# A decoder layer: the order of all engines written out from the first instruction

## The chip, the cores and the metric

The kernel runs on one core of one Trainium2 chip. The metric is the time of one execution in microseconds of the device, median of several runs. A profile is one further execution, recorded by the hardware; its span runs from the first to the last instruction.

The engines are called PE (matmuls), DVE (vector), ACT (activations, scalar), POOL (general) and SP (issues transfers). PEld is PE's loading of weights.

## The reference

One pre-norm decoder layer on x of 32 sequences of 128 tokens, width 128, in float32:

```
x = x + attn(layernorm(x))                 # 16 heads of 8, linear attention: sigmoid(q), sigmoid(k),
                                           # kv = sum k v, num / den, layernorm, gate (h + beta), Wo, relu
x = x + xattn(layernorm(x), ctx_768)       # 16 heads of 64, softmax over 128 context tokens of width 96
x = x + ffn(layernorm(x))                  # a shared SwiGLU, and one of 8 routed experts per token
```

## The kernel before, in words

The 32 sequences are eight groups of four (`x0` to `x7`, tiles of 128 tokens x 4 x 128). For each group there are two short chains and then eight steps:

- `attention(g)`: statistics of x (`st_a`, `mv_a`, `var_a` on DVE, `rstd_a` on POOL), `xn_a`, transposed on PE (`xnTp_a`) and copied by ACT (`xnT_a`); keys and values `kvp` and queries `qp` on PE; the state `stp`, masked into `st_a`; `ndp`, divided into `att`; a second norm (`st_n`, `rstd_n`, `xn_n`, `lnTp`, `lnT`), the gate `hp` and `gT`, `op`, and the sum into x.
- `prologue(g)`: statistics of the new x (`st_b`, `rstd_b`), `xn_b`, transposed (`xnTp_b`, `xnT_b`), and for groups after the first also the context (`eTp`, `eT`).
- the steps. A step is one sequence and one half of the heads of the cross attention, 64 in all. `keys` (`xkp`) and `queries` (`xqp`) of blocks of 128 columns are made four steps ahead into the tiles `qk`; `scores` (`sc`), their maxima (`nmax` on DVE), eight exponentials (`pr` on ACT), `divide` (`rs` on DVE, `pr` times `rs` on POOL), `turn` (`prTa`, `prTb` on PE, copied by DVE and ACT), `values` (`vp`, `v`), `mix` (`avp`, `oT`), `project` (`xyp`, added to x).

The chains are generators that yield a letter at each stage; `place("M", "P")` and the like advance all that wait at such a letter. In the steps every call goes through `InTurn` (line 19), which keeps the order of the program on each engine, by ordering each instruction behind the one before. Ahead of the steps, `InTurn` is off (`on` is set only behind the first queries), and there the scheduler of the framework orders the instructions of each engine by itself. So it is the scheduler that puts `hb_c` ahead of `xn_a` on DVE, that mixes the statistics of two groups, and that sets the second group's `kvp` ahead of the first group's `ndp` on PE.

Before the steps the old program makes all eight keys of group 0 (evicted by ACT), runs `attention(0)` and `prologue(0)`, and `attention(1)` and `prologue(1)` beside them, one stage behind; of group 1 only `eTp`, `xnTp_b` and their evictions are left for step 0.

The loads: SP issues x0, x1, eg0 (the context), wk_x, then small columns (bh, beta, lnw, lnb), wo, bo, wq_x, wv_x, wo_x, bo_x, eg1 and the other x; ACT issues the weights of the first attention (two halves of `wkv_a`, two of `bkv_r`, `wq_a`, `bq_c`). Transfers share a small ring of semaphores, so an issue can wait until an earlier transfer that used the same semaphore has landed.

After the steps come the shared and the routed feed-forward network, which the change does not touch.

Of the kernel before, what the change touches and what calls it, by code (L numbers as in the profile page):

```python
# [12 lines left out]
ALU = mybir.AluOpType  # L13
AX = mybir.AxisListType

P = 128
# [25 lines left out]
def kernel(  # L42
# [31 lines left out]
    nc = tc.nc  # L74
    B, S, D = x.shape
    DE = enc.shape[2]
    INNER = c_wq.shape[1]
# [6 lines left out]
    GT = 4  # L84
# [24 lines left out]
    def bank(name):  # L109
        return ps_mm.tile([P, 512], F32, tag="mm", name=name)  # L110
# [1 line left out]

    xg = []

    def load_x(g):
        t = const.tile([P, GT, D], F32, tag=f"x{g}", name=f"x{g}")
        nc.sync.dma_start(
            out=t, in_=x[g * GT : (g + 1) * GT].rearrange("b s d -> s b d")
        )
        xg.append(t)  # L120

    load_x(0)
    load_x(1)


    ident = const.tile([P, P], F32, tag="ident", name="ident")
# [58 lines left out]
    def column(src, name, queue):  # L185
        t = wa.tile([P, 1], F32, tag=name, name=name)
        queue.dma_start(out=t, in_=src.rearrange("(p o) -> p o", o=1))
        return t
# [6 lines left out]
    def load_e(g):  # L195
        if g < NG:
            t = pe.tile([P, GT, DE], F32, tag="eg", name=f"eg{g}")
            nc.sync.dma_start(
                out=t, in_=enc[g * GT : (g + 1) * GT].rearrange("b s d -> s b d")
            )  # L200
            eg_of[g] = t

    load_e(0)
    wk_x = const.tile([DE, INNER], F32, tag="wk_x", name="wk_x")
    nc.sync.dma_start(out=wk_x, in_=c_wk)
    wh_a = wa.tile([P, D], F32, tag="wh_a", name="wh_a")
    nc.sync.dma_start(out=wh_a, in_=a_wh)
    bh_c = column(a_bh, "bh_c", nc.sync)
    beta_c = column(a_beta, "beta_c", nc.sync)
# [6 lines left out]
    hb_c = wa.tile([P, 1], F32, tag="hb_c", name="hb_c")  # L216

    def late_constants():
        nc.vector.tensor_reduce(
            hsel, ident.rearrange("p (i h) -> p h i", h=HA), AX.X, ALU.add  # L220
        )
        nc.vector.tensor_copy(
            hmask.rearrange("p (i h) -> p i h", h=HA),
            hsel.unsqueeze(1).to_broadcast([P, DA + 1, HA]),
        )
        nc.vector.tensor_tensor(hb_c, bh_c, beta_c, ALU.add)

    wq_x = const.tile([P, INNER], F32, tag="wq_x", name="wq_x")  # L230
# [6 lines left out]
    nc.sync.dma_start(out=bo_x, in_=c_bo.partition_broadcast(P))  # L237
    load_e(1)
    for g in range(2, NG):
        load_x(g)  # L240


    gw_f = const.tile([P, NE], F32, tag="gw_f", name="gw_f")
# [61 lines left out]
    def unordered(ins, done, why):  # L305
# [9 lines left out]
    pe_, dve, act_, pool_ = (  # L315
        InTurn(tc, e) for e in (nc.tensor, nc.vector, nc.scalar, nc.gpsimd)
    )
# [14 lines left out]
    def normalized(src, of, pool, name):  # L332
        mv, rstd = of
        xn = pool.tile([P, GT, D], F32, tag="xn", name=f"xn_{name}")
        for t in range(GT):
            dve.tensor_scalar(
                xn[:, t, :],
                src[:, t, :],
                mv[:, t, 0:1],
                rstd[:, t : t + 1],  # L340
                ALU.subtract,
                ALU.mult,
            )
        return xn

    def transposed(src, n, rows, name):

        ps = bank(name)
        for t in range(n):
            pe_.transpose(ps[0:rows, t * P : (t + 1) * P], src[:, t, :], ident)  # L350
        return ps
# [8 lines left out]
    def attention(g):  # L360
# [66 lines left out]
        for a in range(2):  # L427
            nd2 = bank(f"ndp{g}_{a}")[:, 0 : 2 * W].rearrange("p (b w) -> p b w", b=2)
            for b in range(2):
                t = 2 * a + b  # L430
# [21 lines left out]
        yield "E"  # L452
        an = normalized(att, of, pa, f"n{g}")
        yield "P"
        lnp = transposed(an, GT, P, f"lnTp{g}")
        hp = bank(f"hp{g}")
        pe_.matmul(hp, lhsT=wh_a, rhs=xnT, start=True, stop=True)
        yield "E"
        lnT = pa.tile([P, GW], F32, tag="lnT", name=f"lnT{g}")
        act_.activation(lnT, lnp, AF.Identity, bias=lnb_c, scale=lnw_c)  # L460
# [28 lines left out]
    eT_of, xnT_of, qk_of = {}, {}, {}  # L489

    def encoder(g, evict):

        eT = pe.tile([DE, GW], F32, tag="eT", name=f"eT{g}")
        eT_of[g] = eT
        evict(eT, transposed(eg_of[g], GT, DE, f"eTp{g}")[0:DE, :])
        load_e(g + 2)

    def prologue(g):

        xr = xg[g]  # L500
        yield "S"
        of = statistics(xr, f"b{g}")
        yield "M"
        xn = normalized(xr, of, pe, f"b{g}")

        pool_.tensor_tensor(
            xr, xr, bo_x.unsqueeze(1).to_broadcast([P, GT, D]), ALU.add
        )
        yield "P"
        if g not in eT_of:  # L510
            ep = transposed(eg_of[g], GT, DE, f"eTp{g}")
        xp = transposed(xn, GT, P, f"xnTp_b{g}")
        yield "E"
        if g not in eT_of:
            eT_of[g] = pe.tile([DE, GW], F32, tag="eT", name=f"eT{g}")
            dve.tensor_copy(eT_of[g], ep[0:DE, :])
            load_e(g + 2)
        xnT_of[g] = pe.tile([P, GW], F32, tag="xnT", name=f"xnT_b{g}")
        act_.copy(xnT_of[g], xp)

    def keys(g, s, j, evict):

        cols = slice((4 * s + j) * P, (4 * s + j + 1) * P)
        t = pq.tile([P, 2, GW], F32, tag="qk", name=f"qk{g}_{s}_{j}")
        kp = bank(f"xkp{g}_{s}_{j}")
        pe_.matmul(kp, lhsT=wk_x[:, cols], rhs=eT_of[g], start=True, stop=True)
        evict(t[:, 1, :], kp)
        qk_of[g, s, j] = t

    def queries(g, s, j):  # L530

        cols = slice((4 * s + j) * P, (4 * s + j + 1) * P)
        qp = bank(f"xqp{g}_{s}_{j}")
        pe_.matmul(qp, lhsT=wq_x[:, cols], rhs=xnT_of[g], start=True, stop=True)
        act_.activation(qk_of[g, s, j][:, 0, :], qp, AF.Copy, scale=QSCALE)
# [54 lines left out]
    def divide(k):  # L590
        pr = pr_of[k].rearrange("p a j k -> p (a j) k")
        rs = small.tile([P, 8], F32, tag="rs", name=f"rs{k}")
        dve.reciprocal(rs, sums_of.pop(k))
        pool_.tensor_tensor(
            pr, pr, rs.unsqueeze(2).to_broadcast([P, 8, P]), ALU.mult
        )
# [363 lines left out]
    beside = []  # L960

    def begin(work, then=None):
        beside.append([next(work), work, then])

    def place(*which):
        for at in which:
            for one in list(beside):
                if one[0] == at:
                    one[0] = next(one[1], None)
                    if one[0] is None:  # L970
                        beside.remove(one)
                        if one[2] is not None:
                            begin(one[2]())


    begin(attention(0), lambda: prologue(0))
    place("S")
    late_constants()
    tick = 0
    while beside and 0 not in xnT_of:  # L980
        place("M", "P")
        if tick == 0:
            encoder(0, act_.copy)
            begin(attention(1), lambda: prologue(1))
        else:
            k = tick - 1
            keys(0, k // 4, k % 4, act_.copy)
        place("E", "S")
        tick += 1
    for k in range(tick - 1, 8):  # L990
        keys(0, k // 4, k % 4, act_.copy)
    for j in range(4):
        queries(0, 0, j)

    for engine in (pe_, dve, act_, pool_):
        engine.on = True
    for i in range(len(steps)):
        place("E")
        if i >= 1:
            divide(i - 1)  # L1000
        if i + GT < len(steps):
            if steps[i + GT] not in qk_of:
                keys(*steps[i + GT], dve.tensor_copy)
            queries(*steps[i + GT])
        place("S")
        if i >= 2:
            mix(i - 2)
        scores(i)
        if i >= 3:
            project(i - 3)  # L1010
            if i % 8 == 2:
                begin(router(steps[i - 3][0]))
        place("M")
        if i >= 1:
            turn(i - 1)
        values(i)
        place("P")
        if i % 8 == 3:
            clear_sorted(i // 8)
            g = i // 8 + 2  # L1020
            if g < NG:
                begin(attention(g), lambda g=g: prologue(g))
        if i == 12:
            load_ffn()
        if i == len(steps) - 4:

            first_part.close()
            pools["g"] = ctx.enter_context(tc.tile_pool(name="pg", bufs=2, side="right"))
            pools["c"] = ctx.enter_context(tc.tile_pool(name="pc", bufs=4, side="right"))
            pd = ctx.enter_context(tc.tile_pool(name="pd", bufs=1, side="right"))  # L1030
            pools["down"] = pd.tile([P, NC, NE, D], F32, tag="wdr", name="wdr")
# [10 lines left out]
    n = len(steps)  # L1042
# [136 lines left out]
```

## Time and profile before

| | us |
|---|---|
| median of six runs | 692.55 |
| lowest and highest run | 688.79 and 695.77 |
| the profiled execution | 692.75 |
| its span | 691.0 |
| first matmul starts | 10.23 |
| first matmul of the first scores starts | 44.82 |
| scores of steps 1, 2, 3, 4 start | 50.24, 57.16, 64.08, 71.06 |
| PE busy in the span | 627.8 |

In the timeline a row has the start in us, the duration, the engine, the line, the operation with what it writes and reads, and in brackets the idle time of the engine before it and what ended it. Most operations bear line 30 or 35, the line of `InTurn` that issues them, so rows are told apart by the names of tiles. In the view by stretches, a row has the stretch, its length, and then for PE, PEld, DVE, ACT and POOL the busy time and the number of instructions; behind them the clock granted to PE, the share of the transfer engines that is busy, and GB/s. The granted clock is recorded from its first change on; before that the view shows 1.00.

The chain that ended last runs through PE for 61% of the span, DVE 22%, ACT 7%.

### The profile page before, as it was taken

The page shows a single profiled execution, that of the slowest core. Times are in us where ns is not written, and L with a number is a line of the kernel's source. Part 1 is how long each engine was busy: PE and PEld are TensorE (multiplying, and loading weights), DVE is VectorE, ACT ScalarE, POOL GpSimd, SP SyncE. Part 2 cuts the span into 40 slices and gives each one's busy share as a digit, 9 for nine tenths or more (in the row PEclk, how much of TensorE's full clock was granted, in tenths as well). Part 3 has the DMA queues.
Part 4 walks back from the last instruction along what each step waited for, and adds up shares of the span by engine and source line. Part 5 has one row for each costly group of instructions (what it writes and reads, how often), then busy time and mean ns, then how long its engine had stood idle before and what let it go on. Part 6 is the DMA issues. An engine that isn't in the chain of part 4 may idle for free.

```text
span 691.0 us, 13411 instructions
## 1 busy us (share of the span) xinstructions
PE 627.8 (91%) x4699; PEld 456.8 (66%) x4699; DVE 473.0 (68%) x1265; ACT 335.4 (49%) x1319; POOL 251.5 (36%) x237
## 2 busy tenths in 40 slices
PE   4888999999999999999999999899999789898895
PEld 2545677676667666766676667576766556598873
DVE  3755767878787868786878687867766747444443
ACT  3365654564556465646564557454554531133330
POOL 2132323424342434342424342434252342145552
PEclk9999999999999999999999999999999989899999
DMA  7999700000000000000000000002000000688628
GB/s 178 336 327 371 277 2 1 12 1 9 9 13 1 9 9 12 1 9 9 12 2 13 5 2 1 13 11 56 1 17 1 1 13 5 181 244 251 201 63 219
DMA packets 48258, 50.12 MB, mean 73 GB/s; under 512 B 9232, under 2 KB 33296, under 8 KB 48192
## 3 DMA queue, kind: packets, MB, share of 16 engines
q1 hardware_dynamic: 41888, 42.65, 20.1%
q0 software_dynamic: 2272, 4.72, 2.0%
q10 hardware_dynamic: 4032, 1.90, 1.1%
q8 instruction: 37, 0.61, 0.4%
q14 instruction: 29, 0.24, 0.1%
HBM read 24.60 MB, written 26.76 MB: 74 GB/s over the span
## 4 chain that ended last, share of the span: by engine, by line
PE 61%; DVE 22%; ACT 7%; issue 3%; DMA 2%; SPq 2%; POOL 1%; ACTq 0%; DVEq 0%; POOLq 0%
PE sc L35 8%; PE avp L35 8%; PE xyp L35 6%; ACT pr L35 6%; PE rgu L35 5%; PE xkp L35 5%; PE vp L35 5%; PE xqp L35 5%; DVE nmax L35 4%; PE ryp L35 3%; PE prTa L35 2%; PE prTb L35 2%; DVE x L35 2%; PE kvp L35 2%; SPq L298 1%
## 5 line engine op out<-in xcount | busy, mean ns | idle before, releaser
L35 ACT ACTIVATE pr<-sc,nmax 128x128 f32<-128x128 f32 x512 | 180.1, 378 | 187.7 <-DVE nmax L35 187.1
L35 POOL TENSOR_TENSOR pr<-pr,rs 128x1024 f32<-128x1024 f32 x64 | 121.4, 1896 | 211.7 <-DVE rs L35 78.9
L35 ACT ACTIVATION_READ_ACCUMULATOR pr<-sc,nmax 128x1 f32 x512 | 110.7, 216 | 0.0
L35 PEld LDWEIGHTS avp<-prT,v 128*64 128x64 f32 x1024 | 58.6, 137 | 65.5 <-issue 25.0
L35 PE MATMUL avp<-prT,v 128*64 128x128 f32 x1024 | 77.9, 281 | 13.8 <-ACT prT L35 13.8
L35 DVE TENSOR_REDUCE nmax<-sc 128x8 f32<-128x1024 f32 x63 | 76.9, 1220 | 16.9 <-PE sc L35 16.9
L35 PE MATMUL sc<-qk 64*128 64x128 f32 x1024 | 75.3, 287 | 0.7 <-ACT pr L35 0.7
L35 PE MATMUL xyp<-wo_x,oT 128*128 128x128 f32 x512 | 73.8, 288 | 0.0
L35 PEld LDWEIGHTS sc<-qk 64*128 64x128 f32 x1024 | 62.9, 189 | 13.1 <-issue 10.8
L35 DVE COPY oT<-avp 128x512 f32<-128x512 f32 x64 | 44.0, 688 | 34.6 <-PE avp L35 34.4
L35 PEld LDWEIGHTS xyp<-wo_x,oT 128*128 128x128 f32 x512 | 61.9, 191 | 7.7 <-issue 0.4
L35 PE MATMUL vp<-wv_x,eT 96*128 96x512 f32 x128 | 65.7, 594 | 0.0
L35 PE MATMUL xkp<-eT,wk_x 96*128 96x512 f32 x112 | 58.1, 600 | 7.1 <-DVE eT L35 7.1
L35 PE MATMUL xqp<-xnT_b,wq_x 128*128 128x512 f32 x118 | 60.9, 597 | 0.0
L35 DVE COPY v<-vp 128x512 f32<-128x512 f32 x64 | 43.8, 684 | 18.8 <-PE vp L35 18.7
L35 POOL DMA_INDIRECT xsort<-xs,row x32 | 32.6, 1018 | 58.0 <-issue 38.2
L35 POOL DMA_INDIRECT ytok<-yt,rows x39 | 37.3, 958 | 41.0 <-DVE rows L35 40.7
L35 PE MATMUL prTa<-ident,pr 128*128 128x128 f32 x256 | 38.9, 275 | 11.3 <-POOL pr L35 11.3
L35 ACT ACTIVATE qk<-xqp 128x512 f32<-128x512 f32 x59 | 36.5, 619 | 25.7 <-PE xqp L35 25.7
L35 DVE COPY prT<-prTa 128x512 f32<-128x512 f32 x64 | 43.9, 685 | 6.2 <-PE prTa L35 3.6
L35 DVE COPY qk<-xkp 128x512 f32<-128x512 f32 x56 | 36.5, 651 | 11.6 <-PE xkp L35 11.5
L35 ACT COPY prT<-prTb 128x512 f32<-128x512 f32 x64 | 39.8, 622 | 3.8 <-PE prTb L35 3.8
(213 smaller groups left out, 1009.8 us busy)
## 6 DMA issues: line engine op xcount, KB each, us to landing
xsort<-zeros SPq DMA_DIRECT2D x66, 264.0 KB
wt<-wall SPq DMA_DIRECT2D x39, 256.0 KB
xt<-xsort SPq DMA_DIRECT2D x39, 66.0 KB
x<-in_x_dram SPq DMA_DIRECT2D x8, 256.0 KB
eg<-in_ctx_dram SPq DMA_DIRECT2D x8, 192.0 KB
out_dram<-x SPq DMA_DIRECT2D x6, 256.0 KB
wall<-in_L_ffn_rt_gate_dram SPq DMA_DIRECT2D x1, 1024.0 KB
wall<-in_L_ffn_rt_up_dram SPq DMA_DIRECT2D x1, 1024.0 KB
```

What stands on the lines that cost most here:

```text
L35: self.last = make(*operands, **more)
L298: ins = nc.sync.dma_start(out=xsort[r : r + n].rearrange("(p k) d -> p k d", p=P), in_=zeros)
```

## The change

Four things are changed, all ahead of or in the first steps:

1. `InTurn` is on from the first instruction, so that the order of the program holds on PE, DVE, ACT and POOL from the start. `late_constants` goes through `dve`, and `hb_c` leaves it for a later place.
2. That order is written out call by call. The context's transposes (`encoder`) and key 0 stand first on PE, ahead of the transposes of the first rows; the first group's chain stands in front; keys 1 to 3 and the second group's stages are set between its stages. The second group comes only to its `ndp` before the first queries; the rest of it (`att`, `xn_n`, `hp`, `lnTp`, `gT`, `op`, the whole `prologue(1)`) is put into the list `beside`, and the steps 0 to 3 advance it. Keys 4 to 7 of group 0 are no longer made ahead: steps 0 to 3 make them, as the later steps do, with eviction by DVE.
3. x0 is loaded in two halves, one from SP and one from ACT; wk_x in two halves of columns; x1 goes behind both.
4. In `attention`, `hp` stands ahead of `lnTp`, for all groups.

```diff
-    def load_x(g):
+    def load_x(g, *queues):
         t = const.tile([P, GT, D], F32, tag=f"x{g}", name=f"x{g}")
-        nc.sync.dma_start(
-            out=t, in_=x[g * GT : (g + 1) * GT].rearrange("b s d -> s b d")
-        )
+        n = GT // len(queues)
+        for k, queue in enumerate(queues):
+            queue.dma_start(
+                out=t[:, k * n : (k + 1) * n],
+                in_=x[g * GT + k * n : g * GT + (k + 1) * n].rearrange(
+                    "b s d -> s b d"
+                ),
+            )
         xg.append(t)
-    load_x(0)
-    load_x(1)
+    load_x(0, nc.sync, nc.scalar)
...
-    nc.sync.dma_start(out=wk_x, in_=c_wk)
+    for k in range(2):
+        half = slice(k * INNER // 2, (k + 1) * INNER // 2)
+        nc.sync.dma_start(out=wk_x[:, half], in_=c_wk[:, half])
+    load_x(1, nc.sync)
...
-        nc.vector.tensor_tensor(hb_c, bh_c, beta_c, ALU.add)
...
-        lnp = transposed(an, GT, P, f"lnTp{g}")
         hp = bank(f"hp{g}")
         pe_.matmul(hp, lhsT=wh_a, rhs=xnT, start=True, stop=True)
+        lnp = transposed(an, GT, P, f"lnTp{g}")
...
-    begin(attention(0), lambda: prologue(0))
-    place("S")
+    for engine in (pe_, dve, act_, pool_):
+        engine.on = True
+
+    def whole(g):
+        yield from attention(g)
+        yield from prologue(g)
+
+    def key(k):
+        keys(0, k // 4, k % 4, act_.copy)
+
+    one, two = whole(0), whole(1)
+    next(one), next(two)
+    next(one)
+    encoder(0, act_.copy)
+    key(0)
+    next(one)
+    next(one)
+    next(one)
+    next(two)
+    key(1)
+    next(one)
+    next(one)
     late_constants()
-    tick = 0
-    while beside and 0 not in xnT_of:
-        place("M", "P")
-        if tick == 0:
-            encoder(0, act_.copy)
-            begin(attention(1), lambda: prologue(1))
-        else:
-            k = tick - 1
-            keys(0, k // 4, k % 4, act_.copy)
-        place("E", "S")
-        tick += 1
-    for k in range(tick - 1, 8):
-        keys(0, k // 4, k % 4, act_.copy)
+    next(two)
+    key(2)
+    next(one)
+    next(two)
+    next(one)
+    next(two)
+    key(3)
+    next(one)
+    dve.tensor_tensor(hb_c, bh_c, beta_c, ALU.add)
+    next(two)
+    next(one)
+    next(one)
+    next(two)
+    next(one)
+    next(one)
+    next(two)
+    next(one)
+    next(two)
+    next(one)
+    next(two)
+    next(one)
+    next(one)
+    next(one)
+    next(one)
+    next(one, None)
     for j in range(4):
         queries(0, 0, j)
-
-    for engine in (pe_, dve, act_, pool_):
-        engine.on = True
+    beside.append(["E", two, None])
```

More of the change, by code (lines that the diff above doesn't have):

```diff
@@ L218, in late_constants @@
     def late_constants():
-        nc.vector.tensor_reduce(
+        dve.tensor_reduce(
             hsel, ident.rearrange("p (i h) -> p h i", h=HA), AX.X, ALU.add
         )
-        nc.vector.tensor_copy(
+        dve.tensor_copy(
             hmask.rearrange("p (i h) -> p i h", h=HA),
@@ L239 @@
     for g in range(2, NG):
-        load_x(g)
+        load_x(g, nc.sync)
     gw_f = const.tile([P, NE], F32, tag="gw_f", name="gw_f")
```

## The prediction

> **What bounds the kernel now.** I read the page first, then the timeline of the first 80 us by engine, then PE's busy time and granted clock in short stretches.
>
> ```profile
> span 691.0 us, 13411 instructions
> PE 627.8 (91%) x4699; PEld 456.8 (66%) x4699; DVE 473.0 (68%) x1265; ACT 335.4 (49%) x1319; POOL 251.5 (36%) x237
> ...
> PE   4888999999999999999999999899999789898895
> ```
>
> PE is 91% busy, and from about 70 us on it hardly stops (steps of 7 to 9 us). The change adds and removes no PE work, so it can only gain where PE idles or waits in a wrong order: before the first scores (44.82 us) and in the first steps. Whatever lead exists at step 8 is kept to the end, since the order after that is the same.
>
> Timeline of the stretch before the steps (start, duration, engine, line):
>
> ```profile
> 9.55 0.16 DVE L226 TENSOR_TENSOR hb_c<-bh_c,beta_c 128x1 f32<-128x1 f32 x1 [2.45 <-DMA beta_c<-in_L_attn_beta_dram]
> ...
> 17.80 0.95 DVE L30 TENSOR_TENSOR st_a<-stp,hmask 128x288 f32<-128x288 f32 x2 [2.28 <-PE stp L30]
> ...
> 31.77 1.11 DVE L30 TENSOR_SCALAR xn_n<-att,mv_n,rstd_n 128x128 f32<-128x128 f32 x4 [1.12 <-POOL rstd_n L30]
> ```
>
> ```profile
> 10.23 1.25 PE L30 MATMUL xnTp_a<-ident,xn_a 128*128 128x128 f32 x4 [10.23 <-DVE xn_a L30]
> ...
> 18.09 1.89 PE L30 MATMUL kvp<-wkv_a,xnT_a 128*128 128x256 f32 x8
> 19.82 1.02 PE L30 MATMUL qp<-xnT_a,wq_a 128*128 128x512 f32 x2
> 20.67 1.02 PE L30 MATMUL xkp<-eT,wk_x 96*128 96x512 f32 x2
> 21.54 1.15 PE L30 MATMUL ndp<-st_a,qT_a 128*128 128x144 f32 x8
> ```
>
> Three self-made delays of the first group: DVE sat 2.45 us behind `hb_c`, with `xn_a` behind it; `ndp`, ready at 18.8, stood on PE behind the second group's `kvp`, `qp` and a key until 21.54; `ob`, ready at 31.8, stood on DVE behind the second group's `xn_n` until 32.80.
>
> **Part by part: the way to the first scores.** Durations are pitches, start to start: a 512-column matmul 0.86 us, `kvp` 1.73, `stp`/`ndp` 0.98, `op` 0.88, four transposes 0.44; before 13.5 us PE ran at half of that (an `eTp` transpose 421 ns, at 46 us 272 ns).
>
> - Start to `kvp`. Before: 12.15. After: two halves of x come by two queues, est. 3.8 instead of 4.11; statistics in strict order take 1.9 (group 2 at 70.22 to 72.11), `rstd` 1.04, so `xn_a` starts at 6.7 and not 9.84. But PE now first does `eTp` and key 0, and waits for eg (before: landed about 6.3 behind two x; now behind half an x, est. 5.2), for ACT and for half of wk_x. On ACT, bq_c's issue waits in the built program for wkv_a's first half, which x's half now precedes, so the table load (1.28) starts at est. 5.3 instead of 4.05, and `eT` is copied at 6.6 to 7.2. Key 0 at half rate 1.72: 8.9; `xnTp_a` 0.87 to 9.8; copy 0.6; key 1, 1.72, runs beside it to 11.6. `kvp` at 11.6: **-0.55**. Bounds: eg and wk_x no earlier than before (8.9) gives +1.8; no wait at all -2.0.
> - `kvp` to `ndp`: before 9.39. After: `kvp` 1.73, bias 0.69, `ks` 0.62, `stp`, mask 0.95, key 3: 6.6, part at half rate. **-2.8**.
> - `ndp` to `op`: 9.08 before; without the mixing of `hp`, `lnTp` and `xn_n`, but with strict statistics (+0.3), 8.0. **-1.1**.
> - `op` to `xnTp_b`: 7.35; without `xn_n` (1.0) and the second `gT` in the way 5.8. **-1.55**.
> - `xnTp_b` to `xqp`: 2.36; without key copies in the way on ACT 1.75. **-0.6**.
> - `xqp` to scores: 4.49; one key more on PE: 6 x 0.86 = 5.16. **+0.7**.
>
> Sum -5.9: first scores at 38.9. The other loads cost nothing: wq_x was issued at 9.17 and is needed at 33.8; SP's later waits (x1 on eg, wh_a to lnb on ACT's loads) have 3 to 15 us of slack; if x1 came after 10.5, `kv_a` would be late by as much. POOL's order is unchanged. `hp` ahead of `lnTp` in later groups: 0, `lnT` stands behind exponentials anyway (lnTp done 115.0, lnT at 116.52).
>
> **What the steps give back.** Steps 0 to 3 get four keys (3.44), `hp`, `lnTp`, `op` (2.18); `eTp` and `xnTp_b` go from step 0 to step 3. Step 0: DVE does the second group's statistics before the row maxima: +0.3. Step 1, 6.92 before (scores at 50.24, 57.16): `prTa` starts 2.2 after the scores, then 0.87 + 0.86 + 0.86 + 0.44 + 0.86 + 0.86 + 1.03 = 5.8, so 8.0: +1.1. Step 2: ACT's chain of exponentials still ends last: 0. Step 3, 6.98: PE's first key of group 1 waits for `eT1`, which DVE copies behind `oT`, maxima, `xn_b`, `prT` and `v`, 6.1 after the scores; then 0.86 + 0.86 + 1.03: 8.8, +1.85. Sum **+3.2**. Without a change of clock the lead is 5.9 - 3.2 = **2.7 us**.
>
> **The clock.** Stretches of 3.41 us; columns PE busy, PEld, DVE, ACT, POOL, granted clock:
>
> ```profile
> 34.84:38.25 3.41, 1.43 (x11) 1.25 (x11) 2.15 (x10) 0.59 (x1) 1.01 (x1) 1.00 0.86 267
> ...
> 61.29:64.70 3.41, 1.78 (x26) 1.47 (x26) 0.71 (x2) 2.22 (x10) 1.85 (x1) 1.00 0.99 356
> ...
> 563.05:566.46 3.41, 1.05 (x11) 0.95 (x10) 1.54 (x3) 0.00 (x0) 3.21 (x3) 1.00 0.06 20
> 566.46:569.87 3.41, 3.41 (x6) 0.98 (x4) 0.44 (x1) 1.18 (x2) 1.13 (x2) 0.50 0.12 40
> 586.94:590.35 3.41, 1.26 (x5) 0.57 (x3) 3.17 (x12) 0.60 (x1) 2.50 (x4) 1.00 0.12 40
> 590.35:593.77 3.42, 2.79 (x13) 2.79 (x14) 1.18 (x2) 0.00 (x0) 0.82 (x1) 0.50 0.51 140
> 593.77:597.18 3.41, 3.41 (x7) 1.71 (x7) 0.69 (x1) 0.60 (x1) 0.00 (x0) 0.50 0.63 193
> ```
>
> The half-clock stretches lie on one grid of 3.41 us with the rise at 13.5 us. Twice a stretch with 1.05 and 1.26 us of PE work was followed by half clock; once with 2.79 the half clock stayed; 1.78 kept the full clock. (A third drop, at 552.8, follows a stretch that is busy on paper, with 0.95 us of it `lp`, eight-column matmuls.) The reader should see that sparse PE work costs the *next* 3.4 to 6.8 us.
>
> The keys that the change takes away were PE's filling. In the new order PE has, from the end of `ndp` of group 1 (28.1) to the first `xqp` (33.8), only four transposes, 0.44 us in 5.7. On any grid one stretch there holds under 1.05. So I expect half clock over the six matmuls before the scores: one stretch costs 1.7, two 3.4; the first begins with a wait, like 590.35, so I take **3.3** (0 to 4.3). Again in steps 0 and 1, where PE waits 2 us for the exponentials, does scores (1.09), waits 1.1 for `pr`: about 1.2 in a stretch; this event falls on step 1, now PE-bound: **2.4** (0 to 3.4). In step 0 of before `eTp` and `xnTp_b` filled that hole.
>
> The Trainium skill ("TensorE: Matmul & The Clock Gate", Part 1 and "HAM oscillation") halves PE's clock after a wholly idle window of about 3.4 us and warns of PE gaps above that. By this rule the gap before the scores (3.9 us) trips it and the holes of 1 to 2 us in the steps do not: the sum would be +0.6 instead of +3.0. The rows above trip with 1.05 and 1.26 us of work in the stretch, so I follow them.
>
> Against the profiled execution (692.75 us: span 691.0 and 1.75 around it) the sum is -2.7 + 3.3 + 2.4 = +3.0, 695.75. But its grid was kind to the old order: a stretch began at 10.09, just before the first matmul at 10.23, and the sparse 34.84 to 38.25 (1.43) was cut in two. On another grid the old kernel pays, too: on average 0.85 at the start and some 1.7 to 3.4 in 4 of 10 positions, about 2.1 in all (0 to 3.4). The median of the six runs (692.55, from 688.79 to 695.77) stands for mixed grids: 692.55 + 3.0 - 2.1 = 693.45, rounded to **693.3 us**.
>
> **Rivals.**
> 1. *Lead eaten by steps and clock, no change* (above): 693.3. For it: no PE work goes away; a 5.7 us hole in PE. Against: the thresholds rest on three events. Chance 0.60.
> 2. *The clock holds*, or only one short event comes while the old kernel pays its own: -2.7, with the 2.1 saved -4.8: 687.8 to 689.9. For it: 1.78 busy did not trip. Against: the hole is far emptier than that. Chance 0.20, most of it over 0.5%.
> 3. *Slower by half clock*: both holes cost two full stretches, 2 x 3.4 = 6.8, and the old kernel pays nothing: 692.75 - 2.7 + 6.8 = 696.9. It decides as soon as clock losses exceed 2.7 + 3.5 = 6.2 us beyond those of before. Chance 0.20.
>
> That the order isn't as written is excluded: the built program's queues show it.
>
> **How the numbers follow.** 0.5% (3.46 us) is about what a measurement of this kernel can tell from no change. Faster by more: 0.16, mostly rival 2; slower by more: 0.20, rival 3 and late eg or wk_x (+1.8); between: 0.64. Range 688.4 to 697.0: from the middle of rival 2 to rival 3.
>
> **What would show it.** First matmul at 5 to 5.5 us, `kvp` of group 0 near 11.6, `ndp` near 18, first `xqp` near 33.5; PEclk of about 0.5 somewhere in 31 to 40 and again in 47 to 57; scores at about 42 rather than 39; step 3 of 8.8 us. Wrong if PEclk is 1.00 from 14 us on: then the lead at step 8 is near 2.7. Wrong, too, if key 0 starts after 8.5.

## The result and the profile after

| | before | after |
|---|---|---|
| median, us | 692.71 (80 runs, 688.79 to 695.77) | 694.52 (38 runs, 692.66 to 696.94) |
| ratio to before, 95% interval | | 1.0026 (1.0018 to 1.0034) |
| mean granted clock of an execution, averaged | 0.9894 (30 executions) | 0.9839 (40 executions) |
| first scores start | 44.82 | 41.61 |
| scores of steps 1, 2, 3, 4 | 50.24, 57.16, 64.08, 71.06 | 47.47, 58.50, 65.42, 74.28 |
| profiled execution, its span | 692.75, 691.0 | 693.39, 691.6 |

The change made the kernel 0.26% slower: less than the 0.5% that the chances go by, but outside the interval. The page of the profile after, at the places that were shown of before:

```profile
span 691.6 us, 13415 instructions
PE 630.0 (91%) x4699; PEld 458.4 (66%) x4699; DVE 477.3 (69%) x1269; ACT 333.8 (48%) x1315; POOL 251.4 (36%) x237
...
PE   6689999999899989999999999999998879798895
...
PEclk9978999999999999999999999999999999999999
```

The same instructions on PE are busy 2.2 us longer, and the row of the clock has a dent in its third and fourth slice (34 to 69 us), where before it had none. Timeline of the way to the first scores, DVE and then PE:

```profile
16.16 0.95 DVE L35 TENSOR_TENSOR st_a<-stp,hmask 128x288 f32<-128x288 f32 x2 [0.65 <-PE stp L35]
17.02 0.15 DVE L35 TENSOR_TENSOR hb_c<-bh_c,beta_c 128x1 f32<-128x1 f32 x1
...
27.25 0.69 DVE L35 TENSOR_TENSOR ob<-op,bo_a 128x512 f32<-128x512 f32 x1 [0.52 <-PE op L35]
```

```profile
11.26 1.89 PE L35 MATMUL kvp<-wkv_a,xnT_a 128*128 128x256 f32 x8
...
17.75 1.15 PE L35 MATMUL ndp<-st_a,qT_a 128*128 128x144 f32 x8
...
32.12 1.25 PE L35 MATMUL xnTp_b<-ident,xn_b 128*128 128x128 f32 x4 [3.93 <-DVE xn_b L35]
34.05 5.91 PE L35 MATMUL xqp<-xnT_b,wq_x 128*128 128x512 f32 x8 [0.68 <-ACT xnT_b L35]
39.80 1.02 PE L35 MATMUL xkp<-eT,wk_x 96*128 96x512 f32 x2
...
53.15 1.91 PE L35 MATMUL hp<-xnT_a,wh_a 128*128 128x512 f32 x2
...
71.26 1.12 PE L35 MATMUL xkp<-eT,wk_x 96*128 96x512 f32 x2 [0.98 <-DVE eT L35]
```

The three self-made delays are gone: `hb_c` waits for nothing, `ndp` of the first group stands at 17.75 instead of 21.54, `ob` waits only for its own `op`. The first queries begin 6.28 us earlier (34.05 against 40.33). But the eight passes of the four query matmuls take 5.91 us where before they took 3.70, `hp` in step 1 takes 1.91 where a matmul of that size takes 1.02, and in step 3 PE waits 0.98 for `eT` of the second group.

The view by stretches on this run's own grid of 3.41 us (PE, PEld, DVE, ACT, POOL busy, then the granted clock):

```profile
28.30:31.71 3.41, 0.00 (x0) 0.00 (x0) 2.09 (x10) 0.00 (x0) 1.01 (x1) 1.00 1.00 359
31.71:35.12 3.41, 2.32 (x6) 1.29 (x7) 2.50 (x8) 0.59 (x1) 1.27 (x1) 0.50 1.03 370
35.12:38.53 3.41, 3.41 (x6) 1.34 (x5) 0.00 (x0) 1.19 (x2) 0.00 (x0) 0.50 0.98 312
38.53:41.95 3.42, 3.42 (x14) 1.46 (x14) 1.06 (x4) 1.43 (x3) 0.00 (x0) 1.00 1.01 290
45.36:48.77 3.41, 1.35 (x17) 0.97 (x16) 1.59 (x6) 2.54 (x13) 1.04 (x1) 1.00 1.06 402
48.77:52.19 3.42, 2.51 (x9) 2.10 (x10) 1.82 (x2) 2.25 (x13) 0.85 (x1) 0.50 1.06 387
52.19:55.60 3.41, 3.41 (x8) 1.64 (x7) 0.69 (x1) 1.12 (x5) 0.00 (x0) 0.50 1.06 387
```

Twice PE goes through a sparse stretch (0.00 and 1.35 us of work) and is then granted half clock for two stretches: over the first queries, and over step 1. These are the two clock events of what follows. From 55.6 on the clock is full until 567.6. So the lead that the written order could have at the first scores (predicted 5.9 us; 5.40 in e3 below, where the clock stays full) becomes 3.21, and at the scores of step 4 the new kernel is 3.22 behind.

Behind that it stays behind: the transposes ahead of the last router start at 543.25 before and at 546.51 after. Of these 3.26 us, 2.6 come back in the last fifth, which the change does not touch: there, ahead of the last 2 us, half clock is recorded for 13.65 us before (552.80 to 556.21, 566.45 to 569.87, 590.35 to 597.17) and for 6.83 after. Which stretches fall there differs from run to run, so the single pair of spans (0.6 us apart) says less than the medians (1.8 apart).

### The profile page after: what moved, and what is told of

Read it like the earlier page. It is cut to its first block, busy times and chain, and to the rows that moved or that the text cites. A ratio compares the mean times of both kernels' runs of the same rounds, so it can differ in the third digit from the quotient of the medians.

```text
span 691.6 us, 13415 instructions
## 1 busy us (share of the span) xinstructions
PE 630.0 (91%) x4699; PEld 458.4 (66%) x4699; DVE 477.3 (69%) x1269; ACT 333.8 (48%) x1315; POOL 251.4 (36%) x237
## 4 chain that ended last, share of the span: by engine, by line
PE 61%; DVE 24%; ACT 7%; issue 4%; POOL 2%; DMA 1%; ACTq 0%; DVEq 0%; POOLq 0%
PE sc L35 7%; PE avp L35 7%; PE xyp L35 6%; PE xkp L35 6%; PE xqp L35 5%; ACT pr L35 5%; PE rgu L35 5%; PE vp L35 5%; DVE nmax L35 4%; PE prTa L35 3%; PE ryp L35 3%; PE prTb L35 3%; PE kvp L35 2%; DVE x L35 2%; DVE qk L35 1%
## 5 line engine op out<-in xcount | busy, mean ns | idle before, releaser
L35 PE MATMUL avp<-prT,v 128*64 128x128 f32 x1024 | 76.3, 280 | 11.8 <-ACT prT L35 11.8
L35 PE MATMUL xkp<-eT,wk_x 96*128 96x512 f32 x128 | 68.3, 615 | 8.9 <-DVE eT L35 8.1
L35 PE MATMUL xqp<-xnT_b,wq_x 128*128 128x512 f32 x128 | 67.9, 617 | 0.7 <-ACT xnT_b L35 0.7
L35 PE MATMUL vp<-wv_x,eT 96*128 96x512 f32 x128 | 66.5, 601 | 0.0
L35 ACT ACTIVATE qk<-xqp 128x512 f32<-128x512 f32 x64 | 39.3, 614 | 32.9 <-PE xqp L35 32.8
L35 DVE COPY qk<-xkp 128x512 f32<-128x512 f32 x60 | 39.1, 652 | 19.1 <-PE xkp L35 19.1
L35 PE MATMUL prTa<-ident,pr 128*128 128x128 f32 x256 | 39.8, 279 | 11.7 <-POOL pr L35 11.7
L35 PEld LDWEIGHTS xqp<-xnT_b,wq_x 128*128 128x128 f32 x128 | 24.5, 197 | 33.8 <-issue 24.9
```

Source lines behind the costliest of these rows:

```text
L35: self.last = make(*operands, **more)
```

## The experiments

The theory: the order gains some 6 us up to the first scores; the work moved into steps 0 to 3 gives about 3.2 back; half clock in two holes of PE takes the rest. The rivals: the moved work alone eats the lead, and the clock is incidental; or pieces of the new front (keys ahead of the rows, split loads) cost.

All times are against the kernel before on the same chip; its mean clock was 0.9894 beside e1 to e4, 0.9898 beside e5 to e8 and 0.9901 beside e9 to e12. Gains in per cent are worked out from the ratios. A thousandth of mean granted clock is 0.69 us of a 691 us span at most (less where PE waits anyway).

| | median | ratio to before (95%) | mean clock | first scores | step 1 | step 3 | scores of step 4 |
|---|---|---|---|---|---|---|---|
| before | 692.71 | | 0.9894 | 44.82 | 6.92 | 6.98 | 71.06 |
| after | 694.52 | 1.0026 (1.0018-1.0034) | 0.9839 | 41.61 | 11.03 | 8.86 | 74.28 |
| e1 fill front | 692.28 | 0.9987 (0.9968-1.0006) | 0.9889 | 40.38 | 11.02 | 8.87 | 73.04 |
| e2 fill step | 692.31 | 0.9992 (0.9975-1.0009) | 0.9871 | 42.23 | 8.14 | 9.04 | 72.20 |
| e3 fill both | 690.10 | 0.9956 (0.9937-0.9976) | 0.9909 | 39.42 | 8.14 | 9.05 | 69.38 |
| e4 keys in front | 692.41 | 0.9989 (0.9970-1.0008) | 0.9866 | 41.08 | 9.90 | 9.30 | 72.60 |
| e5 second group early | 691.25 | 0.9978 (0.9964-0.9992) | 0.9883 | 42.76 | 9.12 | 6.97 | 71.73 |
| e6 both of these | 690.33 | 0.9954 (0.9931-0.9978) | 0.9877 | 39.55 | 11.00 | 6.97 | 70.70 |
| e7 rows ahead of keys | 694.19 | 1.0018 (1.0006-1.0030) | 0.9846 | 42.77 | 9.61 | 8.86 | 74.00 |
| e8 before, filled | 690.78 | 0.9976 (0.9957-0.9995) | 0.9934 | 46.25 | 6.91 | 6.98 | 72.55 |
| e9 e6, mended | 686.12 | 0.9918 (0.9892-0.9943) | 0.9928 | 38.12 | 7.01 | 6.98 | 66.90 |
| e10 e9, PE busy from the start | 686.47 | 0.9905 (0.9877-0.9934) | 0.9895 | 38.09 | 7.01 | 6.97 | 67.25 |
| e11 before, hb_c late | 690.32 | 0.9972 (0.9957-0.9986) | 0.9905 | 44.14 | 7.66 | 6.98 | 71.11 |
| e12 after, old loads | 695.89 | 1.0052 (1.0035-1.0069) | 0.9842 | 43.84 | 11.08 | 8.86 | 76.55 |

The last four columns are from one trace each, and the way to `ndp` alone differs by up to 1.4 us between traces of kernels that are the same up to there (17.48 to 18.91, in after, e1 to e6 and e9). It goes with the place of the clock's first rise, which lies anywhere from 10.61 to 13.37 us in these eight, though the first key starts at 6.75 to 7.68 in all of them. A step is from its scores to the next.

### e1, e2, e3: only the holes are filled

```diff
     next(one)
     next(one)
     next(one)
+    spare = big("spare")
+    for k in range(4):
+        pe_.matmul(spare[:, k % 2, :], lhsT=wk_x[:, 0:P], rhs=eT_of[0], start=True, stop=True)
     next(one)
     next(one, None)
```

That is e1. The edit of e2, in `queries`:

```diff
-        pe_.matmul(qp, lhsT=wq_x[:, cols], rhs=xnT_of[g], start=True, stop=True)
+        for _ in range(3 if (g, s, j) == (0, 1, 1) else 1):
+            pe_.matmul(qp, lhsT=wq_x[:, cols], rhs=xnT_of[g], start=True, stop=True)
```

e3 has both edits.

> The changed kernel, with four idle 512-column matmuls added on PE between ndp of the second group and xnTp_b (extra work, written to a bank that nobody reads). It only fills the hole of PE before the first queries. Clock theory: no half clock between 31 and 39 us, the four first xqp at 0.86 us each instead of 1.7, first scores near 38.5 instead of 41.6; the time falls by about 3 us from the 694.5 of the changed kernel, to 691 to 692. The half clock of step 1 stays. Rival (the moved keys and the second group in the steps alone eat the lead, clock incidental): first scores unchanged near 41.6 and 694.5. Rival (the hole would be lost to the added matmuls): xnTp_b later than 32.1.

> The changed kernel, with the sixth query matmul (the one ahead of the second scores) made three times instead of once into the same bank, 1.72 us of extra PE work in the 1.92 us that PE waits there for the exponentials. It only fills the hole of step 0. Clock theory: the half clock of 31.7 to 38.5 stays, that of 48.8 to 55.6 goes, step 1 takes 7.6 to 8 us instead of 11.03; the time falls by about 3 us from 694.5, to 691 to 692. Rival (moved work alone): step 1 keeps 11 us or grows, time 694.5 or up to 1.7 above.

> The changed kernel with both fillings (four idle matmuls before the first queries, two repeated ones before the second scores). Clock theory: granted clock 1.00 from 14 us to beyond 550 us, first scores near 38.5, scores of step 4 near 68 instead of 74.3, which is about 3 us ahead of the kernel before (71.06): 688.5 to 689.5, 0.5 to 0.6% faster than before. Rival (moved work alone): 694.5. If the two halves don't add, the fillings interact.

The stretches of e3 in the same two places:

```profile
28.73:32.14 3.41, 3.07 (x8) 1.05 (x6) 2.08 (x11) 0.00 (x0) 1.01 (x1) 1.00 1.03 373
32.14:35.55 3.41, 2.58 (x8) 1.32 (x9) 2.25 (x8) 0.90 (x2) 1.26 (x1) 1.00 1.03 370
42.38:45.79 3.41, 3.21 (x15) 1.42 (x15) 2.07 (x7) 3.33 (x17) 0.25 (x1) 1.00 0.94 266
45.79:49.21 3.42, 2.37 (x22) 1.77 (x20) 2.14 (x3) 1.47 (x9) 1.64 (x1) 1.00 1.06 401
```

And of its timeline on PE:

```profile
34.07 3.70 PE L35 MATMUL xqp<-xnT_b,wq_x 128*128 128x512 f32 x8 [0.68 <-ACT xnT_b L35]
```

PE does 5.2 us more work than in the changed kernel (six matmuls of 0.86) and the time falls by 0.70% (0.9956 against 1.0026), 4.8 us: the clock stays full from 11.7 to 537 us, and the queries that start at the same time (34.07, 34.05) take 3.70 again. Each filling removes its own event and leaves the other (e1 keeps step 1 at 11.02, e2 keeps the slow queries). By the ratios e1 gives -2.7 us against the changed kernel, e2 -2.4, e3 -4.8: they add, within their intervals. That the moved work alone eats the lead is refuted. e1 misses its numbers for the first scores (38.5 expected, 40.38 found), since its rows came 1.1 us later in that trace; from `xqp` on it takes 5.35 us instead of 7.56. The scores of step 4 in e3 are at 69.38, not near 68 (0.9 of the miss is in the first scores): 1.7 ahead of before. The traced execution of e3 took 693.14 us at a mean clock of 0.987, where the median is 690.10 and the average clock 0.9909: in the last fifth it has half clock from 537.32 to 540.73, 564.62 to 568.04, 588.52 to 595.35 and at the very end, which takes its lead back.

### e4, e5, e6: useful work in the holes

e4 makes keys 4 to 7 where e1 had idle matmuls (`keys` gets an argument `at`, the place in PSUM):

```diff
+    for k in range(4, 8):
+        if k % 2 == 0:
+            two_banks = big(f"xkp_big{k}")
+        keys(0, 1, k % 4, act_.copy, two_banks[:, k % 2, :])
     next(one)
     next(one, None)
     for j in range(4):
         queries(0, 0, j)
```

e5 leaves the keys in the steps, and runs the second group on by three stages before them:

```diff
     next(one)
     next(one)
     next(one)
+    next(two)
     next(one)
     next(one, None)
+    next(two)
     for j in range(4):
         queries(0, 0, j)
-    beside.append(["E", two, None])
+    next(two)
+    beside.append(["P", two, None])
```

e6 has the edit of e5 and these keys:

```diff
+    key(4)
+    key(5)
+    two_banks = big("xkp_big")
+    for k in range(2):
+        keys(0, 1, 2 + k, act_.copy, two_banks[:, k, :])
```

> The changed kernel, with keys 4 to 7 of the first group taken out of steps 0 to 3 and made on PE between ndp of the second group and xnTp_b, copied by ACT; the same work in another place. Clock theory: the first half clock goes (3.3 us), the scores start near 38; the half clock around step 1 stays or comes earlier, since the steps lose 0.86 us of PE work each; time 690 to 692. Rival (the keys in the steps cost by their own 0.86 us, no clock): first scores near 40.8, steps 1 and 3 shorter by 0.86 each, 692.5 to 693.

> The changed kernel, with the second group run on by three of its stages before the loop over steps (att, statistics and xn_n on a DVE that idles from 34.3 to 40.9), so that its hp and lnTp stand in step 0, where PE waits for the exponentials, and all that follows comes one step earlier. The keys stay in the steps. Theory (steps give back 1.1 in step 1 and 1.85 in step 3 because the second group is a step late; its hole in step 0 costs the second half clock): half clock before the first scores stays, the one near step 1 goes, step 1 takes about 7 instead of 11.0 and step 3 about 7 instead of 8.9; scores of step 4 near 68 instead of 74.3; time near 688.5. Rival (steps 0 to 3 are bound by the four keys, whatever stands beside them): step 1 at 8 or more, step 3 unchanged, time 691 or more.

> As e5, and keys 4 to 7 made between ndp of the second group and xnTp_b (two in the banks of the rotation, two in the pair of banks of the scores), so that the hole before the first queries is filled with work that is due anyway. Theory: no half clock between 14 and 500 us, first scores near 38.6, steps of about 6 to 7 us, scores of step 4 near 65 (71.06 in the kernel before); time 684.5 to 687, faster than both. Rival (PE simply has the same work and the end of the program takes the lead back): 690 or more.

e4 came out slower than expected. The first event is gone, as in e1, but three of the four keys wait 0.68 us each for the copy of the one before, so that `xnTp_b` starts at 35.26; and the steps, without the keys, are emptier: the half clock around step 1 stays (47.24 to 54.06). Time and first scores (692.41, 41.08) come near the numbers of its rival (692.5 to 693, 40.8), but not in the rival's way: the first half clock is gone, and step 3 grows to 9.30 instead of losing 0.86.

e5 confirms the part on step 3: with the second group one step earlier it takes 6.97 instead of 8.86 (step 2 takes 7.46 instead of 6.92). The second event is gone, too. Step 1 is the miss, 9.12 where 7 was expected. In e6 the same place, by DVE and PE:

```profile
45.62 0.75 DVE L35 SCALAR_TENSOR_TENSOR gT<-hp,hb_c,lnT 128x512 f32<-128x512 f32 x1 [3.04 <-ACT lnT L35]
46.29 0.19 DVE L35 RECIPROCAL rs<-sums 128x8 f32<-128x8 f32 x1
```

```profile
44.97 1.16 PE L35 MATMUL sc<-qk 64*128 64x128 f32 x16 [1.05 <-ACT pr L35]
48.58 1.12 PE L35 MATMUL prTa<-ident,pr 128*128 128x128 f32 x4 [2.44 <-POOL pr L35]
```

The second group's `gT` now stands on DVE ahead of `rs`, and waits for `lnT`, which ACT makes behind the eight exponentials. `rs` releases POOL, and POOL releases `prTa`: PE waits 2.44 us there instead of 1.05. A stage that is moved earlier has put a wait of its own in front of a chain that ends last. In e6, where the keys are missing from the steps as well, this leaves one sparse stretch, and the half clock is back:

```profile
43.99:47.40 3.41, 1.16 (x16) 0.97 (x16) 1.78 (x3) 2.09 (x8) 0.77 (x1) 1.00 1.04 367
47.40:50.82 3.42, 2.24 (x9) 2.10 (x10) 0.86 (x2) 3.13 (x17) 1.12 (x1) 0.50 1.05 396
```

Both e5 (691.25 against 688.5) and e6 (690.33 against 687 at most) fell short of their numbers mainly for this reason: step 1 is 2.1 and 4 us longer than expected. About 1 us more in each is a later front, and 0.5 and 0.8 us lie in step 2. The traced execution of e6 took 692.37 us at a mean clock of 0.984; three of its nine had 0.992 and took 686.9 to 687.1, so not every execution pays as much.

### e7: the rows ahead of the keys

```diff
     encoder(0, act_.copy)
-    key(0)
     next(one)
     next(one)
     next(one)
     next(two)
-    key(1)
     next(one)
     next(one)
     late_constants()
     next(two)
-    key(2)
+    key(0)
+    key(1)
     next(one)
     next(two)
     next(one)
     next(two)
+    key(2)
     key(3)
```

> The changed kernel, with keys 0 and 1 moved from ahead of and beside xnTp_a to behind the first group's qp, and keys 2 and 3 ahead of its ndp. It sizes what the keys ahead of the rows cost. Theory: key 0 holds xnTp_a by about 1.7 us and key 1 holds kvp by about 0.6, so kvp starts at 9 to 9.5 instead of 11.26; part of it is lost again, since the keys then stand between qp and ndp, and first scores come 1 to 2 us earlier; time 692.5 to 693.5. Rival (PE's clock is still half there, and the keys are its warming up): the full clock comes a stretch of 3.4 us later, kvp takes 3.5 us, ndp not before 17, no gain: 694.5 or more.

```profile
8.87 3.78 PE L35 MATMUL kvp<-wkv_a,xnT_a 128*128 128x256 f32 x8 [0.68 <-ACT xnT_a L35]
12.44 1.26 PE L35 MATMUL qp<-xnT_a,wq_a 128*128 128x512 f32 x2
13.54 1.88 PE L35 MATMUL xkp<-eT,wk_x 96*128 96x512 f32 x4
```

`kvp` starts 2.4 us earlier than after the change (11.26) and takes twice its time (3.57 us to `qp` instead of 1.73), since the clock is half until 12.91; the keys then stand between `qp` and `ndp`, which comes at 18.39, inside the 17.48 to 18.91 of the traces with the keys ahead. Time 694.19, no difference from the change (the intervals overlap); the theory had 692.5 to 693.5. So the keys ahead of the rows cost nothing that these runs can tell, and they fill time at half clock, as the rival has it. That the rise comes a whole stretch later without them isn't shown: 12.91 lies among the rises with the keys ahead.

### e8 and e11: the kernel before, with one thing changed

e8 fills the old kernel's sparse places with repeated work:

```diff
-        pe_.matmul(kp, lhsT=wk_x[:, cols], rhs=eT_of[g], start=True, stop=True)
+        for _ in range(3 if (g, s, j) == (0, 1, 1) else 1):
+            pe_.matmul(kp, lhsT=wk_x[:, cols], rhs=eT_of[g], start=True, stop=True)
...
-        pe_.matmul(qp, lhsT=wq_x[:, cols], rhs=xnT_of[g], start=True, stop=True)
+        for _ in range(2 if (g, s, j) == (0, 1, 1) else 1):
+            pe_.matmul(qp, lhsT=wq_x[:, cols], rhs=xnT_of[g], start=True, stop=True)
```

e11 takes one part of the change alone, `hb_c` behind the first group's mask:

```diff
-        nc.vector.tensor_tensor(hb_c, bh_c, beta_c, ALU.add)
...
-            dve.tensor_tensor(
+            masked = dve.tensor_tensor(
                 st[:, 2 * a : 2 * a + 2, :],
...
+        if g == 0:
+            with tc.issue_after(masked.ins):
+                nc.vector.tensor_tensor(hb_c, bh_c, beta_c, ALU.add)
```

> The kernel before, with key 5 made three times instead of once (1.72 us of extra work, from 34.7 us on) and the sixth query twice (0.86 us, ahead of the second scores), all into the same banks. It tests what the prediction took off for the old kernel, 2.1 us of half clock that it pays on other positions of the grid. If so: 690.5 to 691, mean granted clock higher than that of before by about 0.003. Rival (the old kernel pays next to nothing there, its half clock is all in the last fifth of the run): 692.7 to 693, same mean clock as before.

> The kernel before, with one part of the change alone: hb_c, on which DVE waited 2.45 us, stands behind the first group's mask instead of ahead of xn_a. Theory: xn_a starts at about 7.5 instead of 9.84 and kvp near 10 instead of 12.15, but ndp, standing behind the second group's kvp, qp and a key, and later the mixed stages give most of that back, and the clock takes the rest: first scores 42.5 to 44.5 against 44.82, time 691 to 693 against 692.8. Rival (the wait for hb_c was the whole of what the front could gain): first scores near 42.4 with no half clock added, 690.4.

e8 does 2.6 us more on PE and is 0.24% faster (1.7 us, by its interval 0.3 to 3.0); its mean clock is 0.9934 against 0.9898 of the runs of before beside it, worth up to 2.5 us. Eight of its nine executions have 0.994 or 0.995, and of the 29 of before beside them two. So the old kernel loses about as much clock as the prediction took off for it, and e8 takes most of that away. Where it pays is not settled: in the one trace of each kernel all half clock lies behind 550 us, 13.65 us of it before and 6.83 in e8, ahead of the last 4 us. At the transposes ahead of the last router e8 is 1.4 us behind (544.67 against 543.25), and its gain comes after them. No trace of before or e8 shows the event near 35 to 50 us that the prediction supposed.

In e11 `kvp` comes at 10.01, 2.1 us earlier, `ndp` at 20.85, only 0.7 earlier (it still stands behind the second group's `kvp`, `qp` and a key), and the first scores at 44.14, 0.7 earlier; a stretch of half clock at 51.83 takes the rest, and the scores of step 4 are at 71.11, as before. That is the theory's way. The time, 690.32, is 0.28% (1.9 us) lower all the same, below the theory's 691 to 693, though the mean clock hardly differs (0.9905 against 0.9901). It is the rival's number, without the first scores at 42.4 that the rival gets it from. In the one trace all of it lies in the last fifth: the transposes ahead of the last router start at 543.23 (543.25 before), and the rest is 3.3 us shorter, with 6.8 us less of half clock. The mean clock of the executions doesn't bear that out, so where the gain in time comes from stays open.

### e9 and e10: better than both

e9 mends what the trace of e6 shows (against e6):

```diff
-    key(4)
-    key(5)
     two_banks = big("xkp_big")
-    for k in range(2):
-        keys(0, 1, 2 + k, act_.copy, two_banks[:, k, :])
+    key(4)
+    keys(0, 1, 1, act_.copy, two_banks[:, 0, :])
+    key(6)
+    keys(0, 1, 3, act_.copy, two_banks[:, 1, :])
...
+        if i in (1, 2):
+            divide(i - 1)
         place("E")
-        if i >= 1:
+        if i > 2:
             divide(i - 1)
...
+        if i == 1:
+            values(i)
         if i >= 1:
             turn(i - 1)
-        values(i)
+        if i != 1:
+            values(i)
```

e10 is e9 with PE busy from the start:

```diff
+    cold = const.tile([P, 512], F32, tag="cold", name="cold")
+    nc.vector.memset(cold, 0.0)
+    warm = big("warm")
+    for k in range(2):
+        nc.tensor.matmul(warm[:, k, :], lhsT=cold[:, 0:P], rhs=cold, start=True, stop=True)
```

> As e6, with three mendings of what its trace shows: keys 4 to 7 alternate between a bank of the rotation and the pair of banks (PE waited 0.68 us for a copy); in steps 1 and 2 the reciprocal of the sums stands ahead of the second group's gT on DVE (POOL, and with it prTa, came 1.4 us late); in step 1 the values are made ahead of prTa, in the 1.05 us that PE waits for POOL. Theory: the stretch after the first scores' step now holds about 2 us of PE work instead of 1.1, so no half clock from 14 to 500 us; first scores near 38.6 to 39.5, step 1 near 7 instead of 11, scores of step 4 at 65 to 66.5 against 71.06 in the kernel before; time 685.5 to 688, mean granted clock 0.992 or more. Rival (the remaining hole still trips the clock): half clock near 47 to 54 stays, about 690. Rival (the end of the run takes it back by more half clock there): scores of step 4 at 66, but 690.

> As e9, with two idle 512-column matmuls on a cleared tile at the very start, extra work in the time that PE waits for the first transfer. They only keep PE busy from about 1.5 to 5 us. Theory (full clock follows a nearly full stretch of 3.41 us): the clock rises one stretch earlier, near 8 instead of 11 to 13.5, key 0, xnTp_a, key 1 and kvp take half as long, kvp at 9.5 to 10.3 instead of 11.3 to 12, time 0.7 to 1.7 below e9. Rival (the first eTp waits for the idle matmuls, or the wait for kvp's tables and copies on ACT and DVE sets the pace): kvp at 11 or later and no gain.

The two places in e9:

```profile
31.09:34.51 3.42, 2.25 (x7) 1.04 (x7) 2.95 (x11) 1.21 (x3) 1.60 (x2) 1.00 1.03 372
...
41.33:44.74 3.41, 2.36 (x22) 1.41 (x20) 0.75 (x2) 3.32 (x15) 0.93 (x1) 1.00 1.02 286
44.74:48.16 3.42, 3.42 (x20) 2.21 (x20) 2.53 (x4) 2.05 (x12) 0.96 (x1) 1.00 1.04 364
```

No half clock from 10.6 to 549.9 us, first scores at 38.12, step 1 at 7.01, and at step 4 the lead is 4.2 us (66.90 against 71.06; 65 to 66.5 were expected): 686.12 us, 0.8% faster than before and 1.1% faster than the change. The lead at the first scores, 6.7 us, shrinks in step 2, which takes 9.36 instead of 6.92, mainly since PE waits for the second group's `xn_b`, which DVE makes behind `oT` and the maxima:

```profile
55.83 1.01 PE L35 MATMUL xnTp_b<-ident,xn_b 128*128 128x128 f32 x4 [1.78 <-DVE xn_b L35]
```

The written order is worth 0.8% together with all of this: its holes filled with work that is due anyway, the second group moved ahead, and `divide` and `values` in another order. How much of it each part gives isn't separated.

e10 gets what it is for, and no time from it. PE and then the stretches:

```profile
1.46 3.78 PE L132 MATMUL warm<-cold 128*128 128x512 f32 x4 [1.46 <-DVE cold L129]
...
9.16 2.00 PE L35 MATMUL kvp<-wkv_a,xnT_a 128*128 128x256 f32 x8
```

```profile
29.00:32.42 3.42, 2.25 (x7) 0.85 (x6) 2.62 (x9) 1.57 (x3) 1.96 (x2) 1.00 1.03 377
32.42:35.83 3.41, 3.41 (x5) 1.35 (x4) 2.04 (x12) 1.17 (x2) 1.02 (x1) 0.50 1.04 374
```

The clock rises at 5.11, `kvp` comes 1.8 us before that of e9 and `xnTp_b` 1.7, as the theory has it. But then, in this trace, a stretch with 2.25 us of work is followed by half clock, just over the queries, and the first scores are at 38.09, where those of e9 are. A stretch with the same 2.25 us kept the full clock in e9. A second half clock (56.31 to 59.73) makes step 2 9.76 us. Time 686.47, no difference from e9: its mean clock is lower, 0.9895 against 0.9928, worth up to 2.3 us, which covers the 1.8 of the early start. At a mean clock of 0.994 and 0.995 two executions of e10 took 683.83 and 684.08 us, where three of e9 took 685.62 to 686.42. Whether the early rise brings the further half clock, or six executions of each met it by chance, isn't shown.

### e12: the old loads

```diff
-    load_x(0, nc.sync, nc.scalar)
+    load_x(0, nc.sync)
+    load_x(1, nc.sync)
...
-    for k in range(2):
-        half = slice(k * INNER // 2, (k + 1) * INNER // 2)
-        nc.sync.dma_start(out=wk_x[:, half], in_=c_wk[:, half])
-    load_x(1, nc.sync)
+    nc.sync.dma_start(out=wk_x, in_=c_wk)
```

> The changed kernel with the loads of the kernel before: both x in one piece each from SP, ahead of eg and of wk_x in one piece. It sizes the part of the change that lies in the transfers. Theory: eg lands near 6.3 instead of 4.9 and the whole of wk_x near 8, so key 0 starts near 8 and not at 6.85, and kvp comes 1 to 1.5 us later (12.3 to 12.8), first scores likewise, unless a stretch of half clock shifts; time 694.5 to 696. Rival (the chain is bound by xn_a, and the keys would stand as well behind it): kvp unchanged at 11.3, 694.5.

```profile
6.75 0.42 PE L32 MATMUL eTp<-ident,eg 128*96 128x128 f32 x1 [6.75 <-DMA eg<-in_ctx_dram]
...
8.84 2.05 PE L35 MATMUL xkp<-eT,wk_x 96*128 96x512 f32 x2 [1.02 <-DMA wk_x<-in_L_xattn_Wk_dram]
```

eg lands 1.8 us later (4.94 after the change), key 0 waits for the whole of wk_x, and everything is late by 2.0 to 2.3 us: `kvp` at 13.24, first scores at 43.84. The time is 0.26% (1.8 us) above that of the change. So the loads of the change are worth about that to the order with the keys ahead. Three things differ in them, the halves of x0, the halves of wk_x and x1 behind both instead of ahead of eg; they aren't separated.

## Why the prediction was right, step by step

It said 693.3 (its sum gives 693.45) and no change by its bound (688.4 to 697.0); 694.52 was measured. Its reason, a lead that the steps and the clock eat, is shown by e1 to e3.

| step of the prediction | predicted | measured |
|---|---|---|
| start to `kvp` | at 11.6 | 11.26 |
| `kvp` to `ndp` | 6.6 | 6.49 |
| `ndp` to `op` | 8.0 | 8.30 |
| `op` to `xnTp_b` | 5.8 | 6.07 |
| `xnTp_b` to `xqp` | 1.75 | 1.93 (1.78 in e3) |
| `xqp` to first scores, full clock | 5.16 | 5.35 (e3) |
| first scores, full clock | 38.9 | 39.42 (e3) |
| first half clock, as lost at the first scores | 3.3 | 2.2 (41.61 against 39.42) |
| step 0 | +0.3 | +0.4 (5.86 against 5.42) |
| step 1, full clock | 8.0 | 8.14 (e2, e3) |
| second half clock | 2.4 | 2.9 (11.03 against 8.14) |
| step 2 | 0 | 0.00 |
| step 3 | 8.8 | 8.86 |
| all, at the scores of step 4 | +3.0 | +3.2 |

- That the sum at step 4 is right within 0.2 us is partly luck: errors of +0.5 at the first scores, -1.1 and +0.5 in the two events and +0.3 in the steps nearly cancel. The first rise of the clock was early in this trace, too (11.23); other traces of the same front have `ndp` up to 1.2 us later. That a lead or lag of the first steps is kept to the end holds up to 543 us (3.22 at step 4, 3.26 there), not in the last fifth, where 2.6 of it come back in this pair of traces.
- The front: the gains of its pieces were right within 0.5 us each. The bound for loads that come no earlier than before, +1.8, puts `kvp` at 13.4 if it is counted from 11.6; e12 has it at 13.24. That the keys ahead cost no time beyond what they fill agrees with e7.
- The steps: the four keys and the second group are charged where the prediction put them, step 1 and step 3, and 3.5 us in all instead of 3.2. e5 shows that the 1.9 of step 3 are the lateness of the second group's `eT`, since they go when it is one step earlier, with the key in its old place; 0.5 of them turn up in step 2.
- The clock: both events came where they were expected, each of two stretches. The first was sized too high by 1.1 us: its two stretches of 6.83 us hold 1.1 us in which PE waits anyway, for `xn_b` and `xnT_b`, and at half clock a wait costs nothing. That is worth half of 1.1; where the rest went isn't shown. Over the five traces with this event the first queries take 5.91 to 6.42 instead of 3.70, so it costs 2.2 to 2.7 there. The second was too low by 0.5.
- What the old kernel pays on other positions of the grid: taken as 2.1 us, though its own terms (0.85, and 1.7 to 3.4 in 4 of 10) add up to 1.5 to 2.2. The new kernel lags 3.2 us at step 4 in the traces and 1.8 in the medians, which leaves 1.4 for it. The two events alone are 6.8 us of lost clock, while the mean clocks differ by 0.0055, 3.8 us, so the old kernel loses 3.0 us of clock elsewhere, worth that at most; e8 gives 1.7. So the size holds roughly. The place isn't shown: no trace of the old kernel has half clock near 35 us, and only e11, which is the old kernel but for `hb_c`, has some near the front, at 51.83. Some 0.7 of the 1.2 us by which 693.3 is too low lie in this term.
- The clock holds (rival 2): refuted by every trace of the changed front that leaves its first hole open (after, e2, e5, e7, e12); 34 of 40 executions have the same mean clock of 0.984 as the traced one. e3 shows what it would have given, 690.1, just above that rival's 687.8 to 689.9.
- Slower by half clock (rival 3): its condition was met, both holes cost two full stretches. But of 6.8 us that it charged, only 5.1 were lost, and the old kernel pays too.

On the rule weighed in the prediction: the first event follows a stretch with no PE work at all (28.30 to 31.71), so it fits the rule of the Trainium skill ("TensorE: Matmul & The Clock Gate", Part 1) that a wholly idle window halves the clock. In e7 the same event follows a stretch with 0.61 us of work. The second follows a stretch with 1.35 us of work, so the rule would have missed it, and with it 2.9 us. The measurement decides.

## What to carry to other kernels

When work is taken out of a prologue to shorten its chain, look at what PE has left in each stretch of about 3.4 us: the matmuls that seemed in the way may be what keeps its clock full, and moving them costs the following matmuls up to half of their speed. Fill the waits of a chain with work that is due anyway (e9), and test the suspicion first with idle matmuls, which cost nothing in a hole and show at once what the clock is worth (e3). When a stage is moved ahead, look at each in-order queue that it enters for a wait that it brings with it, such as `gT` ahead of `rs` in e5.

## What was not expected of the hardware

- The bound at which the clock drops is higher than the 1.05 to 1.26 us that the old trace showed. Over the 14 traces, behind the first rise of the clock, every stretch at full clock with at most 1.31 us of PE work was followed by half clock; between 1.35 and 1.68 us it went both ways (kept after 1.66 in e5, lost after 1.65 in e11); above, it was kept in nearly all of them, with drops after 1.80, 1.81, 2.25 and 2.59. The busy time as the profile models it isn't all that decides: the same 2.25 us kept the clock in e9 and lost it in e10.
- A half-clock stretch with at most 2.79 us of work was followed by another (2.32 of 3.41 us in 31.71 to 35.12, 2.51 in 48.77 to 52.19, 2.24 in e6); with 3.21 us or more it was followed by full clock. Between 2.90 and 3.03 it went both ways (full clock after 2.90 in e6, half clock still after 3.00 at the start of e1).
- PE can be brought to full clock at 5.11 us by two idle matmuls of 3.78 us in all, started at 1.46. The rise falls on the grid of stretches, and where the grid lies differs from trace to trace: the same front has its first rise at 10.61 in e9 and at 13.37 in e1. So the order alone doesn't settle which later hole falls into one stretch.
